# Mamba loop on one core: DMA costs by bytes in the planner, and the first image's projections due at step 16 of a tile instead of step 20

## The chip, the cores and the metric

The kernel runs on one core of a Trainium2 chip. The metric is the device time of one execution in microseconds. Before the change the median of three runs was 4532.04 us (4529.59 to 4533.02). The times in this document come from these runs and from one profiled execution, which took 4532.59 us by itself; its span, from its first instruction to its last, is 4530.8 us.

## The reference, cut to what matters

Two images of 256 channels and 64 x 64 = 4096 pixels pass through two layers, each with a group norm ahead and a residual around it, all in fp32.

```python
x = x + mamba_block(_gn(x), ...)      # layer 0
x = x + attention(_gn(x), qkv_w, qkv_b, 8)   # layer 1

# layer 0, y is [B, L, 256], L = 4096
yn = layernorm(y) * gamma + beta
xm, z = split(yn @ W_in.T)            # 512 channels each
u = silu(causal_conv4(xm) + conv_b)
proj = u @ W_xp.T                     # 16 + 16 + 16 columns
dt = softplus(proj[..., :R] @ W_dt.T + b_dt)
Bm, Cm = proj[..., R:R+N], proj[..., R+N:]
# for every step t of L, h is [B, 512, 16]
h = exp(dt_t[:, :, None] * A) * h + (dt_t * u_t)[:, :, None] * B_t[:, None, :]
y_t = einsum('bdn,bn->bd', h, C_t)
ym = (ys + u * D) * silu(z)
y2 = ym @ W_out.T + yn
y3 = gelu(y2 @ W1.T + b1) @ W2.T + b2 + y2

# layer 1: qkv by a 1x1 convolution, 8 heads of 32 channels, softmax over 4096 keys
```

## The kernel before, in words

The kernel has two parts, one after the other. `mamba_stage` computes layer 0 for both images, and also the q, k and v of the first image for layer 1. `attention_block` is then called for each image; its order of work is written out by hand, and the change doesn't touch it.

**Tiles and steps.** `mamba_stage` cuts each image into 8 tiles of 512 pixels (`T`), so there are 16 tiles, numbered 0 to 15. A tile has 32 steps (`STEPS`): 4 groups of 128 channels (`k`), and in each of them 4 groups of states (`qd`) times 2 halves (`quarter`). One step holds two scans of 128 x 512. What is done for a tile has five functions.

- `front(i)` (L470) makes what the scan needs. It loads the image tile into `yn` (L481), normalises it (L479, L493 to L517), projects and convolves it (`conv`, L546), projects dt, B and C (L526 to L540), and computes softplus (`softplus`, L567). There POOL does three passes for each channel group: L594 and L595 for dt, and L597 for the product dt*u. Both results are stored to DRAM (`dt_dram`, `dtu_dram`, L588), and B and C are stored to `bc_dram` (L535).
- `step(g)` (L784) is the scan. `load_rep` (L760, DMA at L767) brings dt and dt*u back from DRAM with each row spread over four partitions (`dt_rep`, `dtu_rep`, 512 KB each, four per channel group); `load_row` (L772, DMA at L779) brings a row of B or C to all partitions (`b`, `c`, 256 KB each, in rings of 4 buffers). ACT computes the decays exp(dt*A) (L803); POOL, in three of four steps, or DVE computes dt*u*B (L809); DVE scans (L814); ACT keeps the last column as the next state (`keep`, L817); POOL multiplies h by C in place (L820), after `keep` has read it; PE sums over the states (L846). There are 512 multiplications at L820 in all, 32 in a tile, and this document counts positions by them: "L820 352" is the last one of tile 10.
- `gate(d, k, due)` (L600) computes silu(z).
- `back(i)` (L611) does the output projection (L621), then the MLP (`up` L643, gelu L646, `down` L657) through the buffer `hid`, adds the residual from `x_back` (loaded at L638), and stores the result into `x_dram` (L671).
- `qkv(b, t, due)` (L674) is called for image 0 alone, once per tile in tiles 8 to 15. It loads the qkv weights and one finished tile of image 0 into `hid` (L686, L687), normalises it (L692), and makes two halves of q and k (ACT at L705, DVE at L709, stored at L714) four times through the same two parts of `hid`, and v (L741, stored at L734).

`hid` has one buffer (`r_hid`), which `back` and `qkv` use in turn.

**What sets the order.** All of this is recorded in a `Plan` (L102). `add(engine, due, cost, emit, reads, writes, tables, lands)` records a task with a due time in steps and a cost in microseconds; `lands` is what passes after a DMA's issue until its data may be used. `order()` (L172) then plays the tasks through: at each moment an idle engine takes, of its tasks whose inputs are ready and whose buffers have room, the one with the earliest due time (a change of ACT's table adds `SWITCH` = 6 to it), and no task more than `HORIZON` = 24 steps beyond the oldest that is still waiting. The cost holds the engine, cost plus lands delays those that read the result. `issue()` emits the tasks in the order found. So costs are never used on the chip; they decide in which order each engine's instructions stand, and on the chip every engine works through its own list in that order, each instruction waiting for its inputs. All DMAs of the stage are issued by SP (`nc.sync`), from one list.

Before the change nearly all DMAs cost 0.8 and land after 2.0 to 4.5, whatever their size:

```python
add("SP", due - 46, 0.8, lambda: nc.sync.dma_start(yn.tile, image_tile(xs[b], t)), [], [yn], lands=4.0)
add("SP", due, 1.6, load, [stored[b * NT + t]], [hid], lands=6.0)
add("SP", g - 7, 0.8, load, [src], [rep], lands=4.5)
```

Image 0's projections are due from `QKV` = 20 steps into a tile (L245, used at L879 and L880).

Of the kernel before, what the change touches and what calls it, by code (L numbers as in the profile page):

```python
# [19 lines left out]
P = 128  # L20
# [81 lines left out]
class Plan:  # L102
# [2 lines left out]

    HANDOVER = 0.2
    TABLE = 1.3
    TABLES = {"exp": "natural_log_exp_and_others", "gelu": "gelu_and_others", "silu": "silu_and_others"}  # L110
# [18 lines left out]
    def add(self, engine, due, cost, emit, reads=(), writes=(), tables=(), lands=0.0):  # L129


        task = Plan.Task()
        task.engine, task.due, task.cost, task.emit = engine, due, cost, emit
        task.tables, task.lands, task.at = tables, lands, len(self.tasks)
        deps = set()
        reads, writes = list(self.keys(reads)), list(self.keys(writes))
        for key in reads:
            deps.add(self.writer.get(key))
        for key in writes:
            deps.add(self.writer.get(key))  # L140
            deps.update(self.readers.get(key, ()))
        for key in reads:
            self.readers.setdefault(key, []).append(task)
        for key in writes:
            self.writer[key], self.readers[key] = task, []
        deps -= {None, task}
        task.deps, task.behind = len(deps), []
        task.ready, task.start = 0.0, None
        for dep in deps:
            dep.behind.append(task)  # L150
        task.bufs = list({id(b): b for b, _ in reads + writes}.values())
        for buf in task.bufs:
            if buf.ring and not buf.left:
                buf.turn = buf.ring.asked
                buf.ring.asked += 1
            buf.left += 1
        self.tasks.append(task)
# [84 lines left out]
SWITCH = 6  # L242
HORIZON = 24

QKV = 20  # L245


@with_exitstack
def mamba_stage(ctx, tc, xs, stats_out, consts, w, outs, scratch):
# [13 lines left out]
    nc = tc.nc  # L263
    ident, gmat, lnmat, eps_t = consts
    IMAGES = len(xs)
    C, L = xs[0].shape
# [203 lines left out]
    def front(i):  # L470

        b, t = divmod(i, NT)
        d = tiles[i]
        due = i * STEPS
        yn = d.yn = Buf(r_yn, KC)

        def norm(k):
            y = yn.tile[:, k, :]
            nc.scalar.activation(y, y, AF.Identity, bias=scales[:, b, k, 0:1], scale=scales[:, b, k, 1:2])  # L479

        add("SP", due - 46, 0.8, lambda: nc.sync.dma_start(yn.tile, image_tile(xs[b], t)), [], [yn], lands=4.0)  # L481
        for k in range(KC):
            add("ACT", due - 41, 0.75, lambda k=k: norm(k), [yn[k], scales_buf[b * KC + k]], [yn[k]])


        mean = Buf(mm)
        add("PE", due - 40, 1.8, lambda: matmul(mean.tile, [(lnmat, yn.tile[:, k, :]) for k in range(KC)]), [yn], [mean])
        sq = [Buf(r_tmp) for _ in range(KC)]
        var = Buf(mm)
        for k in range(KC):  # L490

            def centre(k=k):
                nc.vector.tensor_sub(yn.tile[:, k, :], yn.tile[:, k, :], mean.tile)  # L493

            add("DVE", due - 39, 0.7, centre, [mean], [yn[k]])
            square = lambda k=k: nc.scalar.activation(sq[k].tile, yn.tile[:, k, :], AF.Square)
            add("ACT", due - 38, 0.65, square, [yn[k]], [sq[k], var] if k == 0 else [sq[k]])

        def rstd():

            nc.scalar.activation(var.tile, var.tile, AF.Ln, bias=eps_t)
            nc.scalar.activation(var.tile, var.tile, AF.Exp, scale=-0.5)

        add("PE", due - 37, 1.9, lambda: matmul(var.tile, [(lnmat, s.tile) for s in sq]), sq, [var])
        add("ACT", due - 36, 1.25, rstd, [], [var], ("exp",))
        for k in range(KC):

            def scale(k=k):
                y = yn.tile[:, k, :]
                nc.vector.scalar_tensor_tensor(y, y, gamma[:, k : k + 1], var.tile, ALU.mult, ALU.mult)  # L510

            def shift(k=k):
                y = yn.tile[:, k, :]
                nc.scalar.activation(y, y, AF.Identity, bias=beta[:, k : k + 1])  # L514

            add("DVE", due - 35, 0.75, scale, [var], [yn[k]])
            add("ACT", due - 34, 0.75, shift, [], [yn[k]])  # L517
        d.u = [Buf(r_u) for _ in range(KD)]
        for k in range(KD):
            conv(d, b, k, due - 33 + 4 * k)  # L520

        pp, bc = Buf(mm), Buf(r_bc)
        proj = d.proj = Buf(r_proj)
        d.bc = Buf(parts=1)

        def project():  # L526
            matmul(pp.tile[:NP, :], [(w_xp[:, k, :], d.u[k].tile) for k in range(KD)])

        def halves():
            nc.vector.tensor_sub(proj.tile[LOW:NS, :], pp.tile[:NP, :], proj.tile[:NP, :].bitcast(F32))  # L530

        def store_bc():

            d.bc.tile = dr.tile([2 * N, T], F32, name="bc_dram")
            nc.sync.dma_start(d.bc.tile, bc.tile[R:NP, :])  # L535

        add("PE", due - 14, 3.6, project, d.u, [pp, proj, bc])
        add("ACT", due - 13, 0.6, lambda: nc.scalar.copy(proj.tile[:NP, :], pp.tile[:NP, :]), [pp], [proj])
        add("ACT", due - 13, 0.6, lambda: nc.scalar.copy(bc.tile, pp.tile[:NP, :]), [pp], [bc])
        add("SP", due - 12, 0.8, store_bc, [bc], [d.bc], lands=2.0)  # L540
        add("DVE", due - 12, 0.7, halves, [pp, proj], [proj])
        d.dt, d.dtu = [None] * KD, [None] * KD
        for k in range(KD):
            softplus(d, k, due - 12 + 3 * k + (4 if k else 0))
# [22 lines left out]
    def softplus(d, k, due):  # L567
# [25 lines left out]
        add("DVE", due + 2, 0.7, rest, [pd], [w1])  # L593
        add("POOL", due + 3, 1.27, lambda: nc.gpsimd.tensor_sub(lw.tile, lw.tile, w1.tile), [w1], [lw])  # L594
        add("POOL", due + 3, 1.27, lambda: nc.gpsimd.tensor_add(dt.tile, dt.tile, lw.tile), [lw], [dt])  # L595
        add("SP", due + 3.5, 0.8, lambda: store(d.dt[k], dt, "dt_dram"), [dt], [d.dt[k]], lands=2.0)
        add("POOL", due + 3.5, 1.27, lambda: nc.gpsimd.tensor_mul(lw.tile, dt.tile, d.u[k].tile), [dt, d.u[k]], [lw])  # L597
        add("SP", due + 4, 0.8, lambda: store(d.dtu[k], lw, "dtu_dram"), [lw], [d.dtu[k]], lands=2.0)

    def gate(d, k, due):  # L600

# [9 lines left out]
    def back(i):  # L611
# [23 lines left out]
            )  # L635
        hid = Buf(r_hid, KH)
        xt = Buf(r_xb, KC)
        add("SP", due + 6, 0.8, lambda: nc.sync.dma_start(xt.tile, image_tile(xs[b], t)), [], [xt], lands=4.0)  # L638
        for f in range(KH):
            ph = Buf(mm)  # L640

# [27 lines left out]

            add("DVE", due + 24 + 4 * m, 1.45, end, [acc], [xt[m], stats_bufs[IMAGES + b][m * NT + t]])  # L670
        store = lambda: nc.sync.dma_start(image_tile(outs[b], t), xt.tile)  # L671
        add("SP", due + 29, 0.8, store, [xt], [stored[b * NT + t]], lands=3.0)

    def qkv(b, t, due):  # L674

# [6 lines left out]
        def weights(c, at, n):  # L682
            return flat(0, 3)[:, c * 3 * C + at : c * 3 * C + at + n]

        def load():
            nc.sync.dma_start(flat(0, 3).rearrange("p (k f) -> p k f", k=KC), w["qkv_wT"].rearrange("(k p) f -> p k f", p=P))  # L686
            nc.sync.dma_start(hid.tile[:, 3:5, :], image_tile(outs[b], t))  # L687

        def norm(k):
# [1 line left out]
            sc = scales[:, IMAGES + b, k, :]  # L691
            nc.scalar.activation(x, x, AF.Identity, bias=sc[:, 0:1], scale=sc[:, 1:2])  # L692

        add("SP", due, 1.6, load, [stored[b * NT + t]], [hid], lands=6.0)
        for k in range(KC):
            add("ACT", due + 2, 0.75, lambda k=k: norm(k), [hid[3 + k], scales_buf[(IMAGES + b) * KC + k]], [hid[3 + k]])
        for n, (i, m) in enumerate(((1, 0), (1, 1), (0, 0), (0, 1))):
# [21 lines left out]
            add("PE", at, 1.8, project, [hid[k] for k in range(5)], [pm, *halves])  # L719
            add("ACT", at + 0.5, 0.7, high, [pm], [hid[5]])  # L720
            add("DVE", at + 1, 0.7, low, [pm, hid[5]], [hid[6]])
            add("SP", at + 1.5, 0.8, store, halves, [], lands=3.0)
        for j in range(0, T // P, 2):
            pv = Buf(mm)

            def project(j=j, pv=pv):
                for n in range(2):
                    rows = bass.ts(j + n, P)
                    matmul(pv.tile[:, bass.ts(n, C)], [(hid.tile[:, 3 + c, rows], weights(c, 2 * C, C)) for c in range(KC)])

            def store(j=j):
                for g in range(KG):
                    cs = t * (T // P) + j
                    nc.sync.dma_start(  # L734
                        scratch.v[b * KG + g, :, cs : cs + 2, :],
                        hid.tile[:, 7, :].rearrange("p (n g c) -> p g n c", n=2, g=KG)[:, g],
                    )

            at = due + 4 + 2.2 * j
            add("PE", at, 1.8, project, [hid[k] for k in range(5)], [pv, hid[7]])  # L740
            add("ACT", at + 0.5, 0.7, lambda pv=pv: nc.scalar.copy(hid.tile[:, 7, :], pv.tile), [pv], [hid[7]])  # L741
            add("SP", at + 1, 1.6, store, [hid[7]], [], lands=3.0)


    class Step:
# [14 lines left out]
    def load_rep(g, name, src, ring_):  # L760
# [5 lines left out]
            rows = src.tile.rearrange("(c j) t -> c (j t)", j=QUAD)[:, quarter * T : (quarter + 2) * T]  # L766
            nc.sync.dma_start(rep.tile, rows.unsqueeze(1).to_broadcast([PQ, QUAD, 2 * T]))  # L767

        add("SP", g - 7, 0.8, load, [src], [rep], lands=4.5)
        return rep  # L770

    def load_row(g, ring_, at):  # L772

        i, _, qd, _ = where(g)
        row = Buf(ring_)

        def load():
            src = tiles[i].bc.tile[at + qd * QUAD : at + (qd + 1) * QUAD, :]
            nc.sync.dma_start(row.tile, src.partition_broadcast(PQ))  # L779

        add("SP", g - 5, 0.8, load, [tiles[i].bc], [row], lands=4.0)
        return row

    def step(g):  # L784
# [609 lines left out]
```

## Time and profile before

| | |
|---|---|
| median of three runs | 4532.04 us |
| profiled execution | 4532.59 us, span 4530.8 us |
| busy in the span | PE 4248.6, DVE 3931.0, ACT 3762.3, POOL 3821.2 us |
| PE's granted clock, mean | 0.975 |
| end of the Mamba part (last store issued) | 2120.59 us |
| L820, h times C | 512 times, 2368 ns each |
| L809 on POOL | 384 times, 1279 ns each |
| L594, L595, L597 on POOL | 64 times each, 1278, 1275, 1277 ns |
| L814, scans on DVE | 1024 times, 1273 and 1265 ns |
| ACT table loads in the Mamba part | 338, 1283 ns each |
| `dt_rep`, `dtu_rep` copies | 128 each, 512 KB, median 5.0 and 5.5 us from issue to landing |
| `hid<-in_qkv_wT`, `hid<-x_dram` | 768 and 512 KB, median 5.0 and 6.1 us to landing (1150 to 2000 us) |

The page gives each engine's busy time and its share of the span over all stages, so it doesn't say which engine bounds a stage. For that one takes the busy times of stretches of the span. In the Mamba part the number of instructions per tile is fixed, so a stage is longer only by the idle time of the engine that bounds it; the idle times in the group and wait views name, for each line, what ended the idle time in front of it. An instruction that waited for several things is put down to the one that came last by the profile.

### The profile page before, as it was taken

To read this page: it belongs to the slowest core of one execution; us is meant where nothing else is said; L and a number is where in the kernel's file an instruction comes from. 1 tells how busy PE (TensorE), PEld (TensorE's weight loads), DVE (VectorE), ACT (ScalarE), POOL (GpSimd) and SP (SyncE) were. 2 spreads that over 40 slices of the span, in tenths; PEclk is the share of its full clock that TensorE was granted. 3 is DMA by queue.
4 is the path that set the end of the run, shared out by engine and by line. 5 is a ranking of instruction groups with operands and counts; after the bars stand their busy time and mean duration, and the time that the engine had idled before them with its cause. 6 is when DMAs were issued, how large, how long until landed. Compare 5 with 4: busy or idle time off the path is not lost. (4 is left out here: it accounts for less than half of the span.)

```text
span 4530.8 us, 53988 instructions
## 1 busy us (share of the span) xinstructions
PE 4248.6 (94%) x18530; PEld 1638.8 (36%) x18530; DVE 3931.0 (87%) x3316; ACT 3762.3 (83%) x4836; POOL 3821.2 (84%) x2251
## 2 busy tenths in 40 slices
PE   5799989999899999988999999999899999999998
PEld 2233333333333333333333333333343333333333
DVE  4999989999999899994889889898848898898988
ACT  4788888888788888883999999999739999999997
POOL 2999999999999999994888888888708888888887
PEclk8899999999999999999999999999999999999999
DMA  5233333333443344444311040110091100401100
GB/s 191 96 118 114 108 111 121 126 126 126 143 153 124 127 131 135 153 156 106 88 26 26 20 100 17 26 29 20 20 267 40 45 24 22 101 17 26 28 20 8
DMA packets 172938, 389.24 MB, mean 86 GB/s; under 512 B 24048, under 2 KB 50416, under 8 KB 164464
## 3 DMA queue, kind: packets, MB, share of 16 engines
q1 hardware_dynamic: 172656, 385.73, 28.0%
q8 instruction: 147, 2.41, 0.2%
q14 instruction: 135, 1.11, 0.1%
HBM read 292.34 MB, written 93.32 MB: 85 GB/s over the span
## 5 line engine op out<-in xcount | busy, mean ns | idle before, releaser
L1112 DVE TENSOR_REDUCE chunk<-chunk 128x1024 f32<-128x4096 f32 x288 | 1269.9, 4409 | 226.7 <-ACT chunk L1099 226.7
L1099 ACT ACTIVATE chunk<-s 128x1024 f32<-128x1024 f32 x992 | 1116.7, 1126 | 181.2 <-PE s L1086 146.9
L1153 POOL TENSOR_TENSOR acc_p<-acc_p,e 128x1024 f32<-128x1024 f32 x480 | 1153.0, 2402 | 135.2 <-ACT e L1099 114.1
L1086 PE MATMUL s<-q,k 128*128 128x512 f32 x4096 | 1225.6, 421 | 17.5 <-DMA v<-v_dram 14.8
L820 POOL TENSOR_TENSOR h<-h,c 128x1024 f32<-128x1024 f32 x512 | 1206.5, 2368 | 38.4 <-ACT state L817 27.8
L1120 PE MATMUL po<-chunk,v 128*32 128x512 f32 x3968 | 1114.6, 640 | 0.0
L1120 PE MATMUL po<-e,v 128*32 128x512 f32 x4224 | 1079.0, 605 | 0.0
L1099 ACT ACTIVATE e<-s 128x1024 f32<-128x1024 f32 x1056 | 1069.5, 1016 | 7.4 <-PE s L1086 7.0
L1086 PEld LDWEIGHTS s<-q,k 128*128 128x128 f32 x4096 | 689.8, 188 | 1021.5 <-issue 926.4
L803 ACT ACTIVATE da<-dt_rep,neg_a 128x512 f32<-128x512 f32 x1024 | 690.5, 701 | 118.6 <-DVE h L814 87.7
L1151 POOL TENSOR_TENSOR acc_p<-acc_p,e 128x512 f32<-128x512 f32 x480 | 631.2, 1315 | 161.4 <-ACT e L1099 138.6
L814 DVE TENSOR_TENSOR_SCAN h<-da,state,dbu 128x512 f32<-128x512 f32 x512 | 650.3, 1273 | 52.0 <-POOL dbu L809 45.9
L814 DVE TENSOR_TENSOR_SCAN h<-da,state,bn 128x512 f32<-128x512 f32 x512 | 647.4, 1265 | 12.4 <-POOL dt L595 0.5
L809 POOL TENSOR_TENSOR dbu<-dtu_rep,b 128x512 f32<-128x512 f32 x384 | 486.8, 1279 | 30.8 <-DMA dtu_rep<-dtu_dram 27.9
L234 ACT ACT_TABLE_LOAD x338 | 433.7, 1283 | 6.8 <-PEq L1384 0.7
L425 PE MATMUL bn<-proj,pick 112*128 112x512 f32 x512 | 309.2, 617 | 111.3 <-DVE h L814 111.1
L846 PE MATMUL y<-h,sum 128*32 128x512 f32 x2048 | 358.8, 638 | 24.4 <-POOL h L820 24.0
L809 DVE TENSOR_TENSOR bn<-dtu_rep,bn 128x512 f32<-128x512 f32 x512 | 349.1, 682 | 30.6 <-PE bn L425 16.2
L1150 DVE TENSOR_TENSOR acc<-acc,e 128x512 f32<-128x512 f32 x448 | 309.8, 691 | 24.3 <-ACT e L1099 13.8
L1120 PEld LDWEIGHTS po<-chunk,v 128*32 128x32 f32 x3968 | 142.9, 108 | 360.7 <-issue 349.6
L425 PE MATMUL mm<-yn,w_in 128*128 128x512 f32 x512 | 250.4, 615 | 12.3 <-ACT yn L514 9.3
L425 PE MATMUL mm<-xm,taps 128*128 128x512 f32 x512 | 237.1, 606 | 11.1 <-POOL xm L561 8.7
(135 smaller groups left out, 4068.4 us busy)
## 6 DMA issues: line engine op xcount, KB each, us to landing
dt_rep<-dt_dram SPq DMA_DIRECT2D x128, 512.0 KB, 5.0
dtu_rep<-dtu_dram SPq DMA_DIRECT2D x128, 512.0 KB, 5.5
q<-qk_dram SPq DMA_DIRECT2D x128, 256.0 KB, 4.8
k<-qk_dram SPq DMA_DIRECT2D x64, 512.0 KB, 8.1
b<-bc_dram SPq DMA_DIRECT2D x64, 256.0 KB, 3.1
c<-bc_dram SPq DMA_DIRECT2D x64, 256.0 KB, 4.6
dt_dram<-dt SPq DMA_DIRECT2D x64, 256.0 KB, 2.1
dtu_dram<-lw SPq DMA_DIRECT2D x64, 256.0 KB, 3.4
```

The costliest lines, as they stand in the source:

```text
L234: self.nc.scalar.preload_act_table_set(self.TABLES[task.table])
L425: nc.tensor.matmul(out, lhsT=lhsT, rhs=rhs, start=(i == 0), stop=(i == len(pairs) - 1))
L803: nc.scalar.activation(da[j].tile, dt.tile[:, j, :], AF.Exp, scale=scale)
L809: engine.tensor_mul(out.tile, dtu.tile[:, j, :], rows.tile)
L814: nc.vector.tensor_tensor_scan(h.tile[:, j, :], da[j].tile, dbu.tile, initial, ALU.mult, ALU.add)
L820: nc.gpsimd.tensor_tensor(h.tile, h.tile, rows_c.tile.unsqueeze(1).to_broadcast([P, 2, T]), ALU.mult)
L1086: nc.tensor.matmul(ps[:, j, :], lhsT=keys[i // NT, kt][:, h, kj : kj + P], rhs=queries[i][:, h, :], start=True, stop=True)
L1099: nc.scalar.activation(e, todo[s].s[half], AF.Exp, scale=SCALE)
L1112: nc.vector.tensor_reduce(out, terms, AX.XY, ALU.add)
L1120: nc.tensor.matmul(tiles[i].po[h * D : (h + 1) * D, :], lhsT=v[:, c, g * P + h * D : g * P + (h + 1) * D], rhs=todo[s].e[h // 2][:, h % 2, :],
L1151: nc.gpsimd.tensor_add(acc_p[:, 1, :], acc_p[:, 1, :], eb[:, 1, :])
L1153: nc.gpsimd.tensor_add(acc_p, acc_p, eb)
```

## The change

The cost and `lands` of each DMA are set by its size (512 KB: 1.7 and 3.3; 256 KB: 0.9 and 2.0 or 3.0; smaller ones 0.4 to 1.3). In `Plan.add`, SP tasks due before step 32, which is the first tile and what is prepared in it, get a cost of at most 0.8. In `qkv`, the tile of image 0 is loaded first, due as before, and the weights follow as two DMAs of one half each, due one and two steps later. `QKV` is 16 instead of 20. The line numbers of the changed kernel are up to 9 higher; this document uses those of the kernel before.

```diff
     def add(self, engine, due, cost, emit, reads=(), writes=(), tables=(), lands=0.0):
+        if engine == "SP" and due < 32:
+            cost = min(cost, 0.8)
         task = Plan.Task()
...
-QKV = 20
+QKV = 16
...
-        add("SP", due - 46, 0.8, lambda: nc.sync.dma_start(yn.tile, image_tile(xs[b], t)), [], [yn], lands=4.0)
+        add("SP", due - 46, 1.7, lambda: nc.sync.dma_start(yn.tile, image_tile(xs[b], t)), [], [yn], lands=3.3)
...
-        add("SP", due - 12, 0.8, store_bc, [bc], [d.bc], lands=2.0)
+        add("SP", due - 12, 0.4, store_bc, [bc], [d.bc], lands=1.6)
...
-        add("SP", due + 3.5, 0.8, lambda: store(d.dt[k], dt, "dt_dram"), [dt], [d.dt[k]], lands=2.0)
+        add("SP", due + 3.5, 0.9, lambda: store(d.dt[k], dt, "dt_dram"), [dt], [d.dt[k]], lands=2.0)
...
-        add("SP", due + 4, 0.8, lambda: store(d.dtu[k], lw, "dtu_dram"), [lw], [d.dtu[k]], lands=2.0)
+        add("SP", due + 4, 0.9, lambda: store(d.dtu[k], lw, "dtu_dram"), [lw], [d.dtu[k]], lands=2.0)
...
-        add("SP", due + 6, 0.8, lambda: nc.sync.dma_start(xt.tile, image_tile(xs[b], t)), [], [xt], lands=4.0)
+        add("SP", due + 6, 1.7, lambda: nc.sync.dma_start(xt.tile, image_tile(xs[b], t)), [], [xt], lands=3.3)
...
-        add("SP", due + 29, 0.8, store, [xt], [stored[b * NT + t]], lands=3.0)
+        add("SP", due + 29, 1.7, store, [xt], [stored[b * NT + t]], lands=3.3)
...
+        def load_weights(c):
+            nc.sync.dma_start(weights(c, 0, 3 * C), w["qkv_wT"][c * P : (c + 1) * P, :])
+
         def load():
-            nc.sync.dma_start(flat(0, 3).rearrange("p (k f) -> p k f", k=KC), w["qkv_wT"].rearrange("(k p) f -> p k f", p=P))
             nc.sync.dma_start(hid.tile[:, 3:5, :], image_tile(outs[b], t))
...
-        add("SP", due, 1.6, load, [stored[b * NT + t]], [hid], lands=6.0)
+        add("SP", due, 1.7, load, [stored[b * NT + t]], [hid], lands=3.3)
+        for c in range(KC):
+            w_parts = [hid[0]] if c == 0 else [hid[1], hid[2]]
+            add("SP", due + 1 + c, 1.3, lambda c=c: load_weights(c), [], w_parts, lands=3.0)
...
-            add("SP", at + 1.5, 0.8, store, halves, [], lands=3.0)
+            add("SP", at + 1.5, 1.7, store, halves, [], lands=3.3)
...
-            add("SP", at + 1, 1.6, store, [hid[7]], [], lands=3.0)
+            add("SP", at + 1, 1.0, store, [hid[7]], [], lands=2.5)
...
-        add("SP", g - 7, 0.8, load, [src], [rep], lands=4.5)
+        add("SP", g - 7, 1.7, load, [src], [rep], lands=3.3)
...
-        add("SP", g - 5, 0.8, load, [tiles[i].bc], [row], lands=4.0)
+        add("SP", g - 5, 0.9, load, [tiles[i].bc], [row], lands=3.0)
```

Since costs are known when a program is built, the order in which both programs issue their instructions, engine by engine, can be set side by side without a run. PE, DVE, ACT, POOL and SP have the same work in both, apart from eight DMAs more on SP and six table loads fewer on ACT; the lists stand in another order on every engine from the first tile on.

## The prediction

> **What bounds the kernel now.** I read the slices of the span first, to split it into stages. In the page, POOL is at 9 tenths from slice 2 to slice 18, falls, and comes back at 8:
>
> ```profile
> span 4530.8 us, 53988 instructions
> ...
> POOL 2999999999999999994888888888708888888887
> ```
>
> The planned Mamba loop is the stretch up to about 2121 us; the attention behind it is written out by hand and untouched by the diff. Then the table of busy times by stage (columns: stretch, its length, busy time and count of PE, PEld, DVE, ACT, POOL; granted clock, DMA share, GB/s). The first row is tiles 4 to 8, the second tiles 9 to 15, the third the end of the loop:
>
> ```profile
> 685.00:1161.00 476.00, 440.48 (x1341) 164.73 (x1340) 445.89 (x485) 401.20 (x660) 472.45 (x301) 0.98 0.36 120
> 1161.00:1994.00 833.00, 770.35 (x2395) 305.77 (x2394) 755.05 (x833) 683.41 (x1135) 777.93 (x491) 0.97 0.44 146
> 2085.00:2147.00 62.00, 46.32 (x134) 20.06 (x133) 7.62 (x8) 18.16 (x21) 5.73 (x4) 0.89 0.45 103
> ```
>
> POOL is the bound: idle for 3.55 us in the first row, 55.07 us in the second. DVE is next (94%, then 91%). In the timeline, matching L820 rows are 120.8 us apart in tiles 5 to 8 (678.31, 799.10, 919.87 us) and 128.5 us in tiles 11 to 14 (1418.55, 1547.06, 1676.07, 1804.04 us). The projections of image 0 run only in the later tiles. So what can be won in the loop is some 7.8 us a tile for seven tiles, and one wait of tile 4. The third view says what POOL waits for from 1150 to 2085 us (in total, times, longest):
>
> ```profile
> POOL h L820 <- ACT state L817: 22.6, 24, 3.1
> POOL dbu L809 <- DMA dtu_rep<-dtu_dram: 16.4, 10, 2.5
> POOL h L820 <- issue: 9.0, 7, 1.8
> POOL lw L594 <- DVE tmp L584: 4.6, 4, 2.4
> POOL lw L594 <- DMA hid<-in_qkv_wT: 3.4, 2, 1.9
> ```
>
> Last, the timeline of one tile boundary (start, duration, engine, line; idle before it and releaser):
>
> ```profile
> 1431.71 0.33 SPq L588 DMA_DIRECT2D dtu_dram<-lw  x1
> ...
> 1437.79 1.17 SPq L767 DMA_DIRECT2D dtu_rep<-dtu_dram  x2
> ...
> 1440.34 0.55 SPq L481 DMA_DIRECT2D yn<-in_x  x1
> ...
> 1441.96 1.27 POOL L809 TENSOR_TENSOR dbu<-dtu_rep,b 128x512 f32<-128x512 f32 x1 [2.09 <-DMA dtu_rep<-dtu_dram]
> ...
> 1444.83 1.26 POOL L809 TENSOR_TENSOR dbu<-dtu_rep,b 128x512 f32<-128x512 f32 x1 [1.60 <-PE mm L657]
> ...
> 1447.32 1.52 ACT L479 ACTIVATE yn<-yn,scales 128x512 f32<-128x512 f32 x2 [4.34 <-DMA yn<-in_x]
> ...
> 1453.79 1.26 POOL L594 TENSOR_TENSOR lw<-lw,tmp 128x512 f32<-128x512 f32 x1 [1.86 <-DMA hid<-in_qkv_wT]
> ```
>
> Read it as a chain. The product dt*u (L597) ends at 1431.69; its store lands 6 us later, the two dtu_rep copies (512 KB each) arrive 4.1 and about 7.0 us after that, and POOL stands still 2.09 + 1.60 us. The yn load, issued last, makes ACT stand still 4.34 us; behind it in ACT's queue are L580 and L581, which feed L584 and so POOL's L594: another 1.86 us. (The releasers named for 1.60 and 1.86 us are not the true ones: the second copy and the ACT wait are.)
>
> **The change, part by part.** The edits alter what the planner believes of DMAs, and so the order it writes. The sums below set that order, in both programs, beside durations of the trace; I count positions by the n-th L820. All is summed against the profiled execution (4532.59 us, span 4530.8; median of the runs 4532.04).
>
> First, the dtu_rep copies of a tile's first channel group. Between the end of L597 and the first and second L809 that need them POOL has, before, 8.4 and 9.7 us of other work in tiles 11 to 15 (three L820 of 2.37 and one L809 of 1.28; one L809 more for the second). The waits of tiles 10 to 15 there sum to 3.55 + 3.69 + 4.30 + 3.53 + 2.31 + 1.37 = 18.75 us. After, it is 8.4 and 12.0 us (tile 10: 9.7 and 10.9), and SP's queue changes: two loads of b and c (256 KB each), formerly behind the copies, go ahead of the first; yn (512 KB) goes between the two. The b load must wait for the L809 that frees its buffer, 2.37 + 1.28 = 3.65 us after L597; behind that wait in SP's queue stands the first copy. In tiles 12 and 14 the dt store sits one L820 earlier, so the dt_rep copies have left the queue sooner. I put the copy's issue at 5.5 us after L597 in tiles 11, 13, 15 and 4.5 us in 12, 14 (6.1 now), landing 4.1 us later: waits of 1.2 to 1.7 and 0.2 us. For the second: from 1441.9 to 1447.3 us a copy, b, c and yn landed, 1.5 MB in 5.4 us, 1.8 us per 512 KB; with yn ahead it lands 3.6 to 5 us after the first, and its user comes 3.6 us after: 0 to 1.4 us of wait. Sum about 3 x 2.2 + 2 x 1 = 8.6, say 8: gain 10.5 us. Ends: 18 us, and a loss of 5 if the copy behind yn takes 3 us more.
>
> Second, yn. It now leaves SP ahead of the second copy, b and c, so it lands some 4 us sooner and the 4.34 us ACT wait should go. POOL's waits at L594 (0.69 + 2.35 + 1.86 + 1.52 + 0.73 + 0.82 = 8.0) fall to about 0.7: gain 7.3, ends 3 and 8.
>
> Third, tile 4. Before, that one tile of the quiet half has the short 8.4/9.7 order, and waits 1.57 + 1.32 + 2.84 = 5.7 us; after it has 9.7/10.9, like its neighbours. Those move from 9.7/13.3 with two dt_rep copies ahead to 9.7/10.9 with one ahead; the copy lands one slot earlier and its user 2.4 us earlier, so I book nothing (ends: 0 and a loss of 1 us a tile; the cover is POOL's own queue). Gain 5.7.
>
> Fourth, the projections. QKV 16 instead of 20 moves little: the load waits for the single hid buffer, and stands at L820 353 after, 352 before. The image tile is now loaded ahead of the weights, and its normalise (L692, 2 x 0.76 us) stands one L820 earlier in ACT's queue, ahead of the state copy (L817) that L820 needs. The row of ACT work ahead of that copy at 353 grows to some 8.3 us, against 7.5 us of POOL work; in tiles 11 and 13 two other rows hold two table loads (6.1 and 5.5 us, against 3.8 for a step). No row of before shows these; nothing is the low end if slack covers all, 2 us a tile the high end. The nearest rows, today's waits of 0.6 to 1.2 us behind a table load, give 5 us in all. Table loads fall by six (6 x 1.283 us of ACT, off the path). The weights go as two DMAs, eight issues more at 0.6 us of SP (1.17 for two).
>
> A rule speaks against that split: the Trainium skill's "DMA: Bandwidth & Descriptors" (section "Anatomy of one DMA — SWDGE (gpsimd) path") gives each DMA a fixed 2.0 us plus bytes over 436 GB/s, for that path. By it two halves cost 2 us more a tile, 16 us for eight. The trace has copies issued 0.6 us apart landing about 2.9 us apart while other transfers ran, so queued DMAs overlap; I take 0.6 us a split, hidden, and leave the rule's figure to the range.
>
> Fifth, the end. Before, the last projections' load is issued at 2056.93 to 2057.36 us, and POOL's last L820 is followed by 40.17 us until the attention's first POOL instruction. After, the last L657 and the load stand a little over one L820 later (some 3.5 us), with three of the four serial qk stores behind the last L820, not two. The last image's MLP needs hid, so the end grows: 4 us, ends -2 and 10.
>
> The sum: -10.5 - 7.3 - 5.7 + 5 + 4 = -14.5, so 4532.6 - 14.5 = 4518.
>
> **Rivals.**
> 1. The forecast, about half the DMA waits go: 4518 us. Chance 0.47.
> 2. The more truthful order also takes away ACT's lateness: the 22.6 us at L820 behind L817 fall too, and nothing new comes: 4518 - 5 - 18 = 4495. For it: fewer table loads. Against: the rows ahead of these waits (table load, silu, L817 at L820 332, 340, 345) are the same in tiles 12 and 14. Chance 0.13.
> 3. It hardly does what it says: SP's real rate is set by bytes and buffers, the second copy waits behind yn, and what yn gives is spent there: -10.5 becomes about 0 and the rest stays, 4529. For it: QKV moves nothing, and from 384 to 415 the ACT order is the same in half the rows. Chance 0.27.
> 4. Slower: L692, now one L820 earlier, meets its load too late. Place: ACT at the second L820 of tiles 9 to 15 (353 in tile 11). The page gives hid<-x_dram a median of 6.1 us to landing; L692 is reached some 4 us after the issue I expect, and if the landing took 8.5 us, ACT would wait 4.5 us a tile with L817, the exps and hence L820 behind it: 7 x 4.5 = 31 us in place of 5, 4544. It decides from about (14.5 + 5 + 9) / 7 = 4 us a tile. Against: the load no longer has 768 KB of weights ahead of it. Chance 0.13.
>
> **How the numbers follow.** A measurement of this kernel can tell about 0.2%, 9 us: faster is below 4523, slower above 4541. Rivals 1 and 2 are faster, 3 is the same, 4 is slower: 0.60, 0.27, 0.13. The range reaches from rival 2's size to just under rival 4's: 4495 to 4541.
>
> **What would show it.** L820 rows of tiles 11 to 14 about 126 us apart, not 128.5; POOL's wait for dtu_rep from 1150 us on about halved, that of ACT at L479 for yn nearly gone, L594's with it; no 5.7 us gap near 575 us; 42 to 48 us from POOL's last L820 to the attention. Wrong if waits at L692 or at the second L809 appear, or if the loop gains what the end gives back.

## The result and the profile after

The changed kernel takes 4523.11 us (median of 17 runs, 4517.54 to 4527.64), the one before, run beside it, 4531.48 us (17 runs). The ratio is 0.9981 with a 95% interval of 0.9974 to 0.9988: 8.4 us less (5.4 to 11.8). A few executions of the kernels below ran at a lower granted clock (0.61 to 0.84) and took 5 to 58% longer; they are in no number here. The forecast was 4518 us. The result also lies within 0.2 us of the line (4523) that the prediction drew between faster and the same. The profiled execution after took 4520.82 us (span 4519.0), 11.8 us less in span than before; it is 2.3 us below its median and the one before was 1.1 us above, so 3.4 us of the 11.8 are the scatter of single executions. The time from the last product to the attention scatters far less: the profiles show the same 47.97 to 48.16 us for the changed kernel and for numbers 1, 3, 4 and 8 below, and 40.17 us for the kernel before and number 2. Line numbers are those of each kernel from here on; after, L820 is L829, L809 is L818, L594 is L598, L479 is L483, L692 is L698, L646 is L650.

First the page's slices again, then the first two of the prediction's stretches (length, busy time and count of PE, PEld, DVE, ACT, POOL; granted clock, DMA share, GB/s). Counted by the products, in the kernel before they run from late in tile 4 to late in tile 8, and from there into tile 15:

```profile
span 4519.0 us, 53949 instructions
...
POOL 2999999999999999993888888888608888888887
```

```profile
685.00:1161.00 476.00, 442.67 (x1338) 165.22 (x1338) 445.83 (x485) 400.66 (x661) 471.90 (x300) 0.96 0.35 120
1161.00:1994.00 833.00, 779.38 (x2435) 309.31 (x2436) 769.91 (x851) 690.58 (x1150) 795.61 (x502) 0.98 0.45 149
```

POOL's slices tell the two kernels apart only in slices 19 and 29, by a tenth each. The stretches say more. In the first POOL is idle for 4.1 us, 3.6 before; in the second for 37.4 us instead of 55.1. PE's granted clock is 0.96 and 0.98 in them, 0.98 and 0.97 before. What POOL waits for from 1150 to 2085 us (in total, times, longest):

```profile
POOL h L829 <- ACT state L826: 21.2, 24, 2.7
POOL h L829 <- issue: 6.3, 2, 5.2
POOL dbu L818 <- DMA dtu_rep<-dtu_dram: 6.2, 5, 2.2
...
POOL lw L598 <- DVE tmp L588: 1.1, 2, 0.7
```

The copies' wait fell from 16.4 to 6.2 us, that of L598 from 8.0 (two releasers) to 1.1; ACT's lateness, 22.6 before, is still there. On ACT the wait for yn is nearly gone (before, then after; 1161 to 1994 us):

```profile
ACT yn L479 <- DMA yn<-in_x: 21.2, 5, 4.9
...
ACT yn L483 <- DMA yn<-in_x: 2.3, 4, 0.8
```

The same tile boundary as before (start, duration, engine, line; idle before it and releaser):

```profile
1424.81 0.33 SPq L592 DMA_DIRECT2D dtu_dram<-lw  x1
...
1428.36 0.51 SPq L788 DMA_DIRECT2D b<-bc_dram  x1
1431.00 0.51 SPq L776 DMA_DIRECT2D dtu_rep<-dtu_dram  x1
...
1431.57 0.59 SPq L485 DMA_DIRECT2D yn<-in_x  x1
1432.25 0.52 SPq L776 DMA_DIRECT2D dtu_rep<-dtu_dram  x1
...
1435.76 1.27 POOL L818 TENSOR_TENSOR dbu<-dtu_rep,b 128x512 f32<-128x512 f32 x1 [2.15 <-DMA dtu_rep<-dtu_dram]
...
1439.30 1.27 POOL L818 TENSOR_TENSOR dbu<-dtu_rep,b 128x512 f32<-128x512 f32 x1
```

yn now stands between the two copies. The first copy is still 2.15 us late; the second and L598, 1.60 and 1.86 us late before, wait for nothing.

Last, the end of the loop, before and after:

```profile
2056.93 0.39 SPq L686 DMA_DIRECT2D hid<-in_qkv_wT  x1
...
2067.46 0.69 ACT L705 ACTIVATE hid<-mm,b_qkv 128x512 fp32r<-128x512 f32 x1 [1.84 <-PE mm L425]
...
2078.17 2.35 POOL L820 TENSOR_TENSOR h<-h,c 128x1024 f32<-128x1024 f32 x1 [1.85 <-issue]
...
2092.35 0.69 ACT L646 ACTIVATE hid<-mm,b 128x512 f32<-128x512 f32 x1 [3.35 <-PE mm L425]
...
2120.69 0.12 POOL L940 MEMSET ones<- 128x32 f32 x1 [40.17 <-DVE x_back L667]
```

```profile
2041.40 0.39 SPq L693 DMA_DIRECT2D hid<-x_dram  x1
...
2055.06 0.69 ACT L714 ACTIVATE hid<-mm,b_qkv 128x512 fp32r<-128x512 f32 x1 [4.61 <-PE mm L429]
...
2058.08 2.34 POOL L829 TENSOR_TENSOR h<-h,c 128x1024 f32<-128x1024 f32 x1 [5.15 <-issue]
...
2082.56 1.84 ACT L650 ACTIVATE hid<-mm,b 128x512 f32<-128x512 f32 x3 [2.47 <-DMA qk_dram<-hid]
...
2108.51 0.12 POOL L949 MEMSET ones<- 128x32 f32 x1 [48.09 <-DVE x_back L671]
```

The last POOL product ends at 2060.42 us, 20.1 us sooner than before (2080.52). Counted from there, the first gelu of the last image's MLP, released by the last store of q and k out of `hid`, starts after 22.1 us (11.8 before), and the attention's first POOL instruction after 48.1 us (40.2 before). So the loop gains 20.1 us, and 7.9 of it goes back at its end.

### The profile page after: what moved, and what is told of

Same layout as the page of the kernel before. It is cut to its first block, busy times and chain, and to the rows that moved or that the text cites. A ratio compares the mean times of both kernels' runs of the same rounds, so it can differ in the third digit from the quotient of the medians.

```text
span 4519.0 us, 53949 instructions
## 1 busy us (share of the span) xinstructions
PE 4247.1 (94%) x18530; PEld 1639.2 (36%) x18530; DVE 3926.9 (87%) x3316; ACT 3755.4 (83%) x4830; POOL 3818.5 (84%) x2251
## 5 line engine op out<-in xcount | busy, mean ns | idle before, releaser
L829 POOL TENSOR_TENSOR h<-h,c 128x1024 f32<-128x1024 f32 x512 | 1206.7, 2368 | 40.4 <-ACT state L826 29.4
L812 ACT ACTIVATE da<-dt_rep,neg_a 128x512 f32<-128x512 f32 x1024 | 690.8, 701 | 133.5 <-DVE h L823 107.3
L823 DVE TENSOR_TENSOR_SCAN h<-da,state,dbu 128x512 f32<-128x512 f32 x512 | 650.4, 1273 | 43.2 <-POOL dbu L818 39.9
L823 DVE TENSOR_TENSOR_SCAN h<-da,state,bn 128x512 f32<-128x512 f32 x512 | 646.9, 1264 | 11.6
L818 POOL TENSOR_TENSOR dbu<-dtu_rep,b 128x512 f32<-128x512 f32 x384 | 487.6, 1281 | 17.7 <-DMA dtu_rep<-dtu_dram 13.1
L429 PE MATMUL bn<-proj,pick 112*128 112x512 f32 x512 | 297.5, 597 | 112.0 <-DVE h L823 111.3
L818 DVE TENSOR_TENSOR bn<-dtu_rep,bn 128x512 f32<-128x512 f32 x512 | 348.5, 681 | 39.5 <-PE bn L429 23.0
L429 PE MATMUL mm<-yn,w 128*128 128x512 f32 x512 | 243.9, 606 | 3.2 <-ACT u L562 1.4
```

The lines of the kernel that those rows point to most:

```text
L429: nc.tensor.matmul(out, lhsT=lhsT, rhs=rhs, start=(i == 0), stop=(i == len(pairs) - 1))
L812: nc.scalar.activation(da[j].tile, dt.tile[:, j, :], AF.Exp, scale=scale)
L818: engine.tensor_mul(out.tile, dtu.tile[:, j, :], rows.tile)
L823: nc.vector.tensor_tensor_scan(h.tile[:, j, :], da[j].tile, dbu.tile, initial, ALU.mult, ALU.add)
L829: nc.gpsimd.tensor_tensor(h.tile, h.tile, rows_c.tile.unsqueeze(1).to_broadcast([P, 2, T]), ALU.mult)
```

## The experiments

Theory A: the DMA costs in the planner do it, and step 16 nothing. Its rivals: B, the earlier due time; C, both are needed; D, the image tile loaded ahead of the weights. The first four kernels are meant to tell these apart (the kernel before took 4531.3 us beside them). "Price" and "cost" below mean a DMA's cost and its `lands` together.

**1. The costs alone, step 20.**

```diff
-QKV = 16
+QKV = 20
```

> The changed kernel with QKV back at 20; all DMA costs stay. Theory A, the DMA costs do it and QKV nothing, because the single hid buffer holds the projections' load: within 3 us of the changed kernel, so 6 to 11 us under the kernel before; L820 rows of tiles 11 to 14 about 126.2 us apart, as in the changed kernel. Theory B, the earlier due time does it: within 3 us of the kernel before.

Measured: 4524.57 us, ratio 0.9986 (0.9979 to 0.9994); the end is 48.2 us long. Not told apart from the full change. (In its profile the loop ends 8.2 us later than in the changed kernel, but that execution took 5.6 us more than the median, so a few us for step 16 within the change can't be excluded.)

**2. Step 16 alone, old costs.** The kernel before with `QKV = 16`.

> The kernel before with QKV = 16 and nothing else. Theory A: within 3 us of the kernel before. Theory B: 6 to 11 us under it. If both parts are needed together (theory C), this one and the run with the costs alone each give less than half.

Measured: 4530.75 us, ratio 0.9995 (0.9987 to 1.0004), the end 40.2 us. B falls, and C, which wanted less than half from each, has the costs alone against it. In each of the eight tiles the projections' load is issued at the same product as in the kernel before (the 353rd in tile 11, say): an earlier due time did not bring it forward, since the load waits for `hid`.

**3. Weights first, in one DMA.** The changed kernel with the old load task.

```diff
         def load():
+            nc.sync.dma_start(flat(0, 3).rearrange("p (k f) -> p k f", k=KC), w["qkv_wT"].rearrange("(k p) f -> p k f", p=P))
...
-        add("SP", due, 1.7, load, [stored[b * NT + t]], [hid], lands=3.3)
-        for c in range(KC):
-            w_parts = [hid[0]] if c == 0 else [hid[1], hid[2]]
-            add("SP", due + 1 + c, 1.3, lambda c=c: load_weights(c), [], w_parts, lands=3.0)
+        add("SP", due, 1.6, load, [stored[b * NT + t]], [hid], lands=6.0)
```

> The changed kernel with the projections' load as before: one DMA for the weights, then the image tile, one task of cost 1.6 that lands after 6.0. Theory A: the loop's gain comes from yn and the copies, so the loop keeps 15 us or more of its 20 us gain; L692 again stands one L820 later, and the end is about as long as in the changed kernel (46 to 50 us from POOL's last L820 to the attention's first POOL instruction). Theory D, the image tile ahead of the weights is what helps: the loop loses half of its gain or more, and the time is within 3 us of the kernel before.

Measured: 4526.68 us, ratio 0.9989 (0.9983 to 0.9996). The intervals of this and the full change overlap, so what D is worth is not measured apart. In the one profile of it, an execution 3.8 us above the median, the loop ends 9.3 us sooner than before. A had expected 15 us or more, and half the gain lost was D's sign; D's other sign, a time within 3 us of the kernel before, did not come. POOL's waits behind ACT over the whole loop are 43.5 us (29.4 in the changed kernel). So D may carry part of the gain of the loop where the other costs are new; this stays open. The image tile, behind 768 KB of weights, lands after a median of 7.0 us instead of 3.7, but the normalise doesn't wait longer for it (1.4 us, 1.5 in the changed kernel).

**4. The old cost for yn's load.**

```diff
-        add("SP", due - 46, 1.7, lambda: nc.sync.dma_start(yn.tile, image_tile(xs[b], t)), [], [yn], lands=3.3)
+        add("SP", due - 46, 0.8, lambda: nc.sync.dma_start(yn.tile, image_tile(xs[b], t)), [], [yn], lands=4.0)
```

> The changed kernel with the old cost (0.8, lands after 4.0) for the yn load alone. If it is yn's cost that puts it ahead of the second dtu_rep copy, ACT's wait at L479 for yn comes back (about 4 us in each of tiles 11 to 14) and POOL's wait at L594 with it: 5 to 8 us slower than the changed kernel. If the place of yn follows from the costs of the copies, b and c, nothing moves: within 3 us of the changed kernel.

Measured: 4525.67 us, ratio 0.9988 (0.9981 to 0.9996). POOL's waits at L598 are 0.7 us and ACT's for yn 1.3 us (1161 to 1994 us). yn goes ahead because of what other transfers cost, not because of its own price. Two questions stayed: which price, and what lengthens the end. (For the next four the kernel before took 4534.23 us.)

**5. Old costs for the stores of q, k and v.**

```diff
-            add("SP", at + 1.5, 1.7, store, halves, [], lands=3.3)
+            add("SP", at + 1.5, 0.8, store, halves, [], lands=3.0)
...
-            add("SP", at + 1, 1.0, store, [hid[7]], [], lands=2.5)
+            add("SP", at + 1, 1.6, store, [hid[7]], [], lands=3.0)
```

> The changed kernel with one thing put back: the stores of the projections' results (q and k, and v) have their old costs (0.8 and 1.6 us, seen 3.0 us later) in the planner. In the planner's order the last projections' load then comes two POOL products earlier and the activations of the last full tile's MLP sit where they sat before the change. Theory S (the new store costs stretch the serial q/k chain through the one `hid` buffer in the plan, and this is what made the end 48 us long where it was 40): the stretch from POOL's last product L829 to the attention's first memset falls from 48.1 us to 40 us or less, the loop keeps its 20 us, and the median is near 4516 us. Theory L (the end is long because the loop ends sooner while the data the end needs comes at its old time: the load, the weights and three store-and-reuse rounds of hid take what they take): the stretch stays at 46 to 49 us and the median within 3 us of 4523 us.

Measured: 4519.03 us, ratio 0.9968 (0.9956 to 0.9980). The loop ends at 2060.08 us as in the changed kernel, and the end is shorter:

```profile
2077.88 1.84 ACT L650 ACTIVATE hid<-mm,b 128x512 f32<-128x512 f32 x3 [2.52 <-DMA qk_dram<-hid]
...
2103.83 0.12 POOL L949 MEMSET ones<- 128x32 f32 x1 [43.75 <-DVE x_back L671]
```

S holds for 4.3 of the 7.9 us; neither expectation had a figure between. By the times alone, the intervals of this and the full change overlap. The load is issued at 2031.35 us, 10 us sooner, but the four rounds through `hid` then take 9.7, 9.9 and 8.6 us from one high half (L714) to the next, so the first gelu is only 4.7 us sooner.

**6. No projections in the last tile.** Those of image tiles 1 and 2 are made in one tile of the loop.

```diff
-        if 0 <= t < NT:
+        if 0 <= t < NT - 1:
...
-            qkv(0, t, (i + 1) * STEPS + QKV)
+            for j in {0: (0,), 1: (1, 2)}.get(t, (t + 1,)):
+                qkv(0, j, (i + 1) * STEPS + QKV + 12 * (t == 1 and j == 2))
```

> The changed kernel, but the first image's projections of sub-tiles 1 and 2 are both put into the same tile of the loop, so that those of the following ones come one tile sooner and the last tile of the loop has none. All work stays. If the end is long because the last image's MLP waits for `hid` until the projections of the last tile have stored q and k (theories S and L alike), the stretch from the last L829 to the attention's memset falls from 48.1 us to 30 to 35 us, at a price of 0 to 6 us in the tile that does two sets of projections: median 4508 to 4516 us, below both kernels. If the end is bound by something else (the MLP's own matmuls, gelus and stores, about as long as it is already), the stretch stays above 43 us and the median is 4520 us or more.

Measured: 4528.98 us, ratio 0.9990 (0.9982 to 0.9998), where 4508 to 4516 us was expected if `hid` alone held the end. Both expectations of the end were too simple:

```profile
2090.01 0.69 ACT L650 ACTIVATE hid<-mm,b 128x512 f32<-128x512 f32 x1 [14.18 <-PE mm L429]
...
2118.35 0.12 POOL L950 MEMSET ones<- 128x32 f32 x1 [41.35 <-DVE x_back L671]
```

With `hid` free the end still takes 41.35 us: the first gelu comes 13.0 us after the last product, released by PE, and the memset 28.3 us after that. We read this as the chain of output projection and MLP itself. The kernel before stood on it too (11.8 + 28.3 = 40.2 us), so its last projections cost its end nothing. In the changed kernel `hid` comes late and PE has meanwhile worked ahead (three gelus run without a wait, where before ACT waits 1.03 us for PE ahead of each), and the memset follows the first gelu after 26.0 us: 22.1 + 26.0 = 48.1. In this kernel the tile with two sets of projections and its neighbours pay for the move: POOL's waits in tiles 10 and 11 (1321 to 1583 us) rise to 24 us, from 10 in the changed kernel.

**7. The old price for the dt_rep and dtu_rep copies.**

```diff
-        add("SP", g - 7, 1.7, load, [src], [rep], lands=3.3)
+        add("SP", g - 7, 0.8, load, [src], [rep], lands=4.5)
```

> The changed kernel with the planner's cost of the two broadcast copies of 16 steps (dt_rep and dtu_rep) put back to 0.8 us, landing after 4.5 us; every other cost as changed. If the gain at the tile boundaries comes from these copies' own cost (a dearer copy lets the planner see that SP's queue fills, so that the next tile's b, c and dtu_rep copies are spread and started in time), POOL's waits for dtu_rep in the loop go back from 10.7 to about 20 us and the median to 4528 to 4532 us. If it comes from what the other loads and stores cost (image tiles and weights at 1.7 us and 1.3 us), the waits stay near 11 us and the median near 4523 us.

Measured: 4547.10 us, ratio 1.0028 (1.0017 to 1.0039): slower than the kernel before, which neither expectation had. POOL's waits at L818 are 12.2 us over the loop, 10.7 in the changed kernel and 23.5 before; what rose is the wait behind ACT (first fence, 1150 to 2085 us). On ACT the normalise of the image tile meets its load too late in every tile (second, 1161 to 1994 us), and that load lands after 7.1 us in the median instead of 3.7 (third, the DMA view: KB each, us to landing):

```profile
POOL h L829 <- ACT state L826: 55.3, 46, 3.2
```

```profile
ACT hid L698 <- DMA hid<-x_dram: 20.1, 7, 4.0
```

```profile
hid<-x_dram SPq DMA_DIRECT2D x7, 512.0 KB, 7.1
```

SP's lists say why. Here, in six of the seven tiles, two dtu_rep copies of 512 KB go out within 2.9 us ahead of that load, a c load of 256 KB 0.7 to 1.0 us ahead, and the weights 1.0 to 1.3 us after it; the load lands after 6.4 to 8.5 us, and L698 starts 6.4 to 8.6 us after the load's issue. In the changed kernel, in tiles 11 to 15, the last copy goes out 4.5 us or more ahead, the weights follow after 1.8 to 3.8 us, the load lands after 3.7 to 4.0 us, and L698 finds its tile there 4.7 to 6.1 us after the issue. From 1150 to 2085 us ACT waits 19.4 us more at L698 than in the changed kernel, and POOL 34.1 us more behind ACT; the rest of POOL's loss was not traced. At the end of tile 3, where the changed kernel had got rid of tile 4's waits for the copies, POOL waits 3.6 us for them again (4.2 before).

**8. The first tile priced by bytes too.**

```diff
-        if engine == "SP" and due < 32:
-            cost = min(cost, 0.8)
```

> The changed kernel without its exception: SP's tasks of the first tile too cost what their bytes say. The stretch before the first product gets no cheaper by it: if the exception matters as its author's choice implies, the first product L829 starts 2 to 6 us later and the median is 4525 to 4529 us; if costs of the first tile move nothing that POOL waits for, the median is within 2 us of 4523 us. A side question: the three first tiles lost 2.8 us in all with the change; if that came from the exception's edge (costs that jump at step 32), it goes and the median falls to 4520 us.

Measured: 4529.46 us, ratio 0.9991 (0.9983 to 1.0000). The time did not fall, so the side question is answered with no. The first product starts no later (99.1 us, after 100.0), so the reason given for the loss was wrong, though the size is close: tile 0 lasts 134.0 us instead of 118.0, tiles 1 and 2 win 10 us of it back, and the loop ends 9.1 us later.

**9. The copies' price alone.** The kernel before, which took 4532.53 us beside this and the next, with two edits:

```diff
+        if engine == "SP" and due < 32:
+            cost = min(cost, 0.8)
...
-        add("SP", g - 7, 0.8, load, [src], [rep], lands=4.5)
+        add("SP", g - 7, 1.7, load, [src], [rep], lands=3.3)
```

> The kernel before with one part of the change alone: the two copies of 16 steps (dt_rep and dtu_rep) cost 1.7 us in the planner instead of 0.8 and land after 3.3 us instead of 4.5, with the first tile left out of it; all other costs, the single weights load and step 20 stay. Theory R (the copies' cost alone spreads SP's list at the tile boundaries): POOL's waits for dtu_rep fall from 23.5 to 11 us or less, those for ACT stay near 29 us, and the median is 4518 to 4525 us. Theory M (the gain comes only where all transfers are priced alike, since pricing some of them high lets the others be put ahead of them): the waits for ACT or for a load rise as they did where the copies alone kept the old price, and the median is 4530 us or more.

Measured: 4518.70 us, ratio 0.9971 (0.9960 to 0.9982). R holds in the time and in the copies. POOL's waits from 1150 to 2085 us (L823 is the product by C, L812 dt*u*B):

```profile
POOL h L823 <- ACT state L820: 29.2, 31, 3.2
POOL dbu L812 <- DMA dtu_rep<-dtu_dram: 7.6, 5, 2.5
```

The copies' wait halves (16.4 before), and that at the softplus pass, 8.0 us before, is 0.7 us for the whole loop. So both of the prediction's first two steps, the copies and yn, come from this one price. R had expected the waits behind ACT to stay near 29 us; over the whole loop they rose from 27.8 to 38.8 us, a part of what M expected, and the gain came in spite of it. The edit shortens what the planner lets pass from a copy's issue to its use only from 5.3 to 5.0 us, but holds SP for 1.7 us instead of 0.8; the two were not tried apart. Put in a square with numbers 1 and 7 (time by that of the kernel before):

| | copies at 0.8 | copies at 1.7 |
|---|---|---|
| other costs old | 1 | 0.9971 |
| other costs new | 1.0028 | 0.9986 |

The copies' price is worth 13 us with the old costs around it and 19 with the new. The square isn't quite clean: number 7 stands at step 16, the other three at 20, and "other costs new" includes the split load with the image tile first. The other costs together lose 13 us with cheap copies and some 7 with dear ones, where the intervals just overlap. With dear copies the profiles put the difference at the end (number 9, then number 1):

```profile
2108.80 0.12 POOL L943 MEMSET ones<- 128x32 f32 x1 [42.06 <-DVE x_back L670]
...
2116.74 0.12 POOL L949 MEMSET ones<- 128x32 f32 x1 [48.16 <-DVE x_back L671]
```

That is 6.1 us, while from the first product to the last the two take 1966.3 and 1966.7 us.

**10. Number 5, with `hid` free sooner.** For the next to last tile the second matmuls of the MLP are due 6 to 7 steps earlier, with the sums and the store behind them (number 5's lines and those of the sums and the store are left out here).

```diff
-                add("PE", due + 19 + 4 * m + f / 2, 2.7 if f == 0 else 1.8, lambda f=f, down=down: down(f), reads, [acc])
+                add("PE", due + (19 + 4 * m if i != 2 * NT - 2 else 13 + 3 * m) + f / 2, 2.7 if f == 0 else 1.8, lambda f=f, down=down: down(f), reads, [acc])
...
```

> The kernel with the old store costs (4519.0 us, 43.8 us from the last L829 to the attention's memset) with one more edit: the second matmuls of the next to last tile's MLP, which hold hid until the last projections can load it, are due 6 to 7 steps earlier. In the planner's order the last load then comes one POOL product (some 3.8 us) earlier. If hid alone sets the end, the stretch falls by 2 to 4 us to 40 to 42 us, where the chain of w_out, MLP and store takes over (41.35 us without any projections in the last tile), and the median is 4515 to 4518 us. If the earlier matmuls delay the scan's own sums on PE, the loop gives that back and the median stays at 4518 to 4522 us.

Measured: 4514.84 us, ratio 0.9962 (0.9949 to 0.9975), the lowest median of all, 17 us below the kernel before; the intervals of this and number 5 overlap. The end:

```profile
2075.72 1.84 ACT L650 ACTIVATE hid<-mm,b 128x512 f32<-128x512 f32 x3 [2.44 <-issue]
...
2101.67 0.12 POOL L949 MEMSET ones<- 128x32 f32 x1 [42.02 <-DVE x_back L671]
```

It is 1.7 us shorter than number 5's and 0.7 us from what it was without any projections there. The loop gave nothing back (2059.65 us).

## Why the prediction was right, and where it was not

The forecast of 14.5 us less was right in its mechanism and too high: 11.8 us by the profiles, 8.4 by the medians. By the time alone the result stands halfway between the forecast (4518) and rival 3 (4529); the profiles decide between them. The steps in turn, by the two profiles:

- **Copies at the boundaries.** Forecast -10.5, measured -8.6 (all of POOL's waits at L809, now L818, went from 23.5 to 10.7 us in the loop; 4.2 us of that fall is tile 4's). At the boundaries of tiles 10 to 15 themselves the 18.75 us fell by 11.3 to 7.4; the forecast left 8. The second copies bring 8.4 of it, the first ones 3.0: the copy behind yn came in time in tiles 11 to 13 and 0.42 us late in tile 14, so rival 3's mechanism did not occur. But 3.3 us came new in the middle of tiles 12 and 14, behind DVE's scan, which the forecast had at nothing; why was not traced.
- **yn.** Forecast -7.3, measured -6.9.
- **Tile 4.** Forecast -5.7, measured -4.2 at the copies and -1.6 at L829.
- **Projections and ACT's packing.** Forecast +5; POOL's waits at L829 outside tile 4 rose by 2.9. Table loads hardly changed (in tiles 9 to 15, 135 and 133). That step 16 moves little was right (number 2).
- **The end.** Forecast +4, measured +7.9. This is the term that was mis-sized. The step counted only that the load comes some 3.5 us later relative to the last product; it came 4.6 us later (19.0 us ahead of that product's end, 23.6 before). It left out that the chain behind it gets longer: 3.1 us more from the load to the first high half, which waits 4.61 us for PE, and 2.6 us more from there to the first gelu. That makes 10.3, of which the MLP, with PE ahead of it, saved 2.4. That three stores of q and k would stand behind the last product, not two, was right.

The signs that the prediction named were there: the products that the prediction followed (128.5 us apart before) are 125.6 us apart in the mean, 1411.64 to 1788.37 us (126 forecast), and the gap near 575 us is gone. These rows are those of tiles 10 to 13, not 11 to 14 as it says, and its other three are those of tiles 4 to 6.

The loop's four steps sum to -18.4 us measured, -18.5 forecast; that they agree so well is luck, since single steps miss by some 2 us each way. With +7.9 that is -10.5; the first product started 0.8 us sooner and 0.5 us lies in other small differences, which makes 11.8.

**The rivals.** Rival 2 is refuted: ACT's lateness is 21.2 us. Rival 4 did not occur: L698 waits for its load once, 1.5 us. But its mechanism is real: number 7 has it in all seven tiles, 20.1 us in sum where the rival had 31. That its 4544 us come so near number 7's 4547 us is partly chance, for the rest of that loss was not traced. In the changed kernel it was held off by the price of the copies, which keeps them away from the load; the argument given against it, that 768 KB of weights no longer stand ahead of the load, was not enough, since they don't in number 7 either.

**The split of the weights.** By the Trainium skill's "DMA: Bandwidth & Descriptors" ("Anatomy of one DMA — SWDGE (gpsimd) path") with its fixed 2.0 us a DMA, given for DMAs that GpSimd issues, the eight additional DMAs of the split would cost 16 us, an estimate that takes them one after another. These are issued by SP and queued: in the changed kernel the second half leaves 0.5 to 0.8 us behind the first and lands 0.8 to 1.0 us behind it, in all eight pairs, so 2.0 us more are not seen there. Number 3 takes the split and the order of the loads back together, and is not faster (3.6 us slower by the medians, not resolved). A split by itself was not tried.

**What the forecast did not ask** is which of the edits carries the gain. It treated the prices as one edit with one answer. One price brings all of it (number 9), and the rest of the change adds nothing that can be told from noise; at the end it costs 6.1 us (numbers 9 and 1), 4.3 of it from the prices of the q, k and v stores (number 5). The largest loss is 13 us from the other prices with cheap copies (number 7). We read it so that prices act by their ratio within one queue: where the others rose and the copies' did not, the copies went out close ahead of a load that ACT waited for. That is a reading of two orders, not a rule; number 9 too raises only one price, and gains.

## What to carry to other kernels

Where an order comes from a planner, take its costs one at a time: here one cost of eleven carried the gain, and the others, more truthful too, brought nothing more and lost 13 us without it. Before booking what a loop gains, write down what its end waits for and how much slack each of those chains has; here the loop ended 20 us sooner, but the load into the one buffer `hid` came only 15.5 us sooner and its chain took longer, and 8 us were lost. A mechanism that a profile does not show may be one price away: look what holds it off before calling it unlikely.

## What the runs showed of the hardware that was not expected

The time that a 512 KB load takes depends on what SP issued around it. `hid<-x_dram` landed after 3.7 to 4.0 us where the last copies had gone out 4.5 us earlier or more (tiles 11 to 15 of the changed kernel), and after 6.4 to 8.5 us where two 512 KB copies had gone out within 3 us ahead and the weights followed within 1.3 us (six tiles of number 7). So the planner's fixed 1.7 + 3.3 = 5.0 us is 1.0 to 1.3 us too long for a load with the queue to itself, and 1.4 to 3.5 us too short for one in a crowd. Whether the engines of the DMA or the memory are shared there was not tested.
